# A gated cross-attention, feed-forward and slot-expert block: half of the slots attend among the experts' products

## The chip, the cores and the metric

The kernel runs on one core of a Trainium2 chip. The metric is the device time of one execution, in microseconds (us). Everything is float32. A core has five engines that run their own instruction streams in order: TensorE (PE in the profile; PEld is its weight load), VectorE (DVE), ScalarE (ACT), GpSimd (POOL) and SyncE (SP, which here only issues DMAs). Sixteen DMA engines move the data.

## The reference, cut to what matters

```python
# x, ctx: (8, 512, 512); 4096 tokens of width 512
x = x + tanh(g_xattn) * xattn(layernorm(x), ctx, mask)
x = x + tanh(g_ffn) * ffn(layernorm(x))

def xattn(x, context, mask):            # 16 heads of 64; keys and values shared by all heads
    xn, cn = layernorm(x) * gamma, layernorm(context) * ctx_gamma
    q, (k, v) = heads(xn @ Wq) / 8, split(cn @ Wkv)
    attn = softmax(where(mask == 0, -inf, q @ k.T))
    out = merge(attn @ v) @ Wout
    a, gate = split(xn @ Wff1)          # 2048 each
    return out + (silu(gate) * a) @ Wff2

def ffn(x):                             # 16 slots, one expert each, F = 2048
    q = broadcast(slot_query)
    o = q + mha(q, x, x)                # slots attend to the 512 tokens; 16 heads of 32
    h = layernorm(o)
    u, g = silu(h @ e_W1[slot] + b1), silu(h @ e_Wg[slot] + bg)
    o = o + (u * g) @ e_W2[slot] + b2
    return mha(x, o, o)                 # tokens attend to the 16 slots
```

## The kernel before

The eight batches of 512 tokens go through five stages, one after the other.

**A, cross-attention (lines 145 to 685).** A unit is a batch, a half of the heads and a block of 128 queries: 8 x 8 = 64 units, numbered by g. The loop of line 586 takes two steps (h) for a unit. `scores` multiplies keys with queries on PE (L292), takes the row maximum on DVE (L303), the exponential on ScalarE (L306) and normalises on POOL (L319). `turn_blocks` (L331) transposes 32x32 blocks on DVE, and one unit later `spread` (L335) moves the blocks to their partitions with sixteen DMAs of 128 KB on SP's queue; for the last two units every second one is on POOL's. `weigh` (L349) multiplies with the values, `add_out` (L365) with Wo. The keys of a batch are needed on both halves of the partitions: `place_keys` (L252) copies one half to the other by a DMA on SP (L258). Before the loop starts, for the first batch, the two loads of Wo (1 MB each, L557) stand ahead of that copy on SP. In the last batch there is no next batch to prepare, and PE takes steps of `carried_queries` (L379) instead: it folds the slots' queries with their key weights into the tile qt.

**B, feed-forward (lines 699 to 1052).** Products of combined blocks (L806, L830), with combinations made by POOL and DVE. Its first loads (xs, w1g, w1a; L737 to L744) are on SP, behind the last `spread`.

**C, the slots attend (lines 1111 to 1264).** 16 slots x 16 heads make 256 rows of queries in qt, two blocks m = 0, 1 of 128 rows. For each batch: `turn_tokens` (16 transposes on PE, copied to the tile places[b] by ScalarE and DVE), `slot_scores` for each m (four matmuls with 512 columns, then DVE's maximum, ScalarE's exponential, DVE's reciprocal, POOL's normalising), `turn_probs` (four transposes for each m, copied by ScalarE), `slot_pool` (16 matmuls of 256 columns). After the last batch, 64 small and 4 large matmuls per output (L1254, L1261) make o for all 128 rows (slot, batch).

**D, the experts (lines 1268 to 1456).** 16 experts, each with 8 pieces of 1 MB of W1 and Wg (4 matmuls on each) and 4 pieces of W2 (4 matmuls): 192 pieces. `fetch` (L1077) issues the next piece on SP as soon as a piece's matmuls free its buffer. There are RING = 8 buffers that are filled in stage C, and MORE = 2 that come free at its end. The products of an expert are small on PE: all eight batches' slot makes 8 rows, padded to 32. Beside them run the tokens' queries of stage E: `token_queries` (L1346), 128 steps of one matmul with 512 columns, one after each piece of W1 and Wg from the second expert on. The order on PE is written out by hand: `open_expert` (biases), `expert_in`, `turn_hidden` of the expert before, `gate` on ScalarE and DVE, `expert_out` of the expert before, with `close_group` every fourth expert.

**E, the tokens attend to the slots (lines 1466 to 1597).** Starts when the last expert is in.

Each engine takes its instructions in the order of the program; PE cannot pass a step that waits.

Of the kernel before, what the change touches and what calls it, by code (L numbers as in the profile page):

```python
# [26 lines left out]
P = 128  # L28
# [10 lines left out]
NS = 16  # L39
NE = 16  # L40
# [9 lines left out]
def flamingo_block(  # L50
# [45 lines left out]
    qt = const.tile([P, ND, FH * NS], F32, name="qt")  # L96
# [48 lines left out]
    with ExitStack() as sa, tc.manual_schedule(engines=ALL_ENGINES):  # L145
# [106 lines left out]
        def place_keys(b, kp, made):  # L252
            kT = a2.tile([P, N], F32, tag="kT", name=f"kT_{b}")
            v = a2.tile([P, NT, XD], F32, tag="v", name=f"v_{b}")
            nc.scalar.copy(kT[0:XD, :], kp[0:XD, :])
            vT = a3.tile([P, N], F32, tag="cn", name=f"vT_{b}")
            nc.scalar.copy(vT[XD:P, :], kp[XD:P, :])
            nc.sync.dma_start(kT[XD:P, :], kT[0:XD, :])  # L258
            made["kT"] = kT
            yield  # L260
            tp = ps1.tile([P, NT, XD], F32, tag="turn", name=f"v_tp_{b}")
            for t in range(NT):
                nc.tensor.transpose(
                    tp[:, t, :], vT[XD:P, t * P : (t + 1) * P], ident[XD:P, XD:P]
                )
            nc.scalar.copy(v, tp)
            made["v"] = v
            yield
# [14 lines left out]
        def scores(b, u, pairs, qs, kT, bias, turned, behind):  # L283
# [39 lines left out]
            for l in pairs:  # L323
                for e in (0, 1):
                    behind.append((turned, 2 * l + e, prs[l, e]))
# [9 lines left out]
        def spread(b, u, turned):  # L335
# [3 lines left out]
            last = b == B - 1 and u >= UNITS - 2  # L339
            for k in range(4):  # L340
                for i in range(4):

                    queue = nc.gpsimd if last and i % 2 else nc.sync
                    queue.dma_start(  # L344
                        pT[32 * k : 32 * k + 32, :, i, :], src[32 * i : 32 * i + 32, :, k, :]
                    )
            return pT

# [30 lines left out]
        def carried_queries():  # L379
# [27 lines left out]
            bdq = a4.tile([P, 4, 4, NS], F32, tag="xn", name="bdq")  # L407
            nc.vector.memset(bdq, 0.0)
            for r in range(4):
                s = slice(FD * r, FD * r + FD)  # L410
                nc.vector.tensor_tensor(bdq[s, :, r, :], qp[s], wide(dbqT[s], NS), ALU.add)
            yield
            for g in range(4):
# [7 lines left out]
                for c in range(ND):  # L421
                    nc.tensor.matmul(
                        tp[:, c, :], lhsT=wkT[:, c * P : (c + 1) * P],
                        rhs=bdq[:, g].rearrange("p r s -> p (r s)"), start=True, stop=True,
                    )
                nc.vector.tensor_copy(qt[:, :, g * 64 : (g + 1) * 64], tp)
                yield
            tp = ps1.tile([P, 2], F32, tag="turn", name="bk_tp")
            for g in range(4):
                r0 = 64 * (g % 2)  # L430
                nc.tensor.matmul(
                    tp[r0 : r0 + 64, g // 2 : g // 2 + 1],
                    lhsT=bdq[:, g].rearrange("p r s -> p (r s)"), rhs=dbkT[:, g : g + 1],
                    start=True, stop=True,
                )
# [121 lines left out]
        for hp in range(2):  # L557
            nc.sync.dma_start(
                wo[:, hp * HP : hp * HP + HP], rows(Wout[hp * HP * P : (hp + 1) * HP * P, :])
            )  # L560
# [25 lines left out]
        for h in range(2 * (B * UNITS + 3)):  # L586
# [35 lines left out]
            if h == 1:  # L622
                next(kv)
            if h == 4:
# [5 lines left out]
            if k == 0 and to_spread is not None:  # L630
                sb_, su, st_, sv = to_spread
                to_weigh_next = (sb_, su, spread(sb_, su, st_), sv)
# [24 lines left out]
            if k == 1 and to_weigh is not None:  # L657
                for _ in weigh(*to_weigh, done):
                    pass
            if live and nb < B:  # L660
# [395 lines left out]
    RING, MORE = 8, 2  # L1056
# [5 lines left out]
    fetched = []  # L1062
    pieces = []
    for e in range(NE + 1):
# [4 lines left out]
        if e > 0:  # L1069
            for q in range(4):  # L1070
                pieces.append(("w2", e - 1, q))

# [4 lines left out]
    def fetch():  # L1077
# [3 lines left out]
        pool, tag = buffers[len(fetched) % (RING + MORE)]  # L1081
        t = pool.tile([P, 4, 512], F32, tag=tag, name=f"{kind}_{e}_{i}")
        fetched.append(piece)
# [14 lines left out]

# [6 lines left out]
    ball = slots.tile([P, 2, 256], F32, name="ball")  # L1105

# [3 lines left out]

    with ExitStack() as sc, tc.manual_schedule(engines=ALL_ENGINES):
        c1 = sc.enter_context(tc.tile_pool(name="c1", bufs=1, reuse_waits="tile"))
        c2 = sc.enter_context(tc.tile_pool(name="c2", bufs=2, reuse_waits="tile"))
        ps = sc.enter_context(tc.tile_pool(name="ps_c", bufs=2, space=PSUM, reuse_waits="tile"))

        dbo = c1.tile([P, D], F32, tag="mT", name="dbo")
        pooled = c1.tile([P, ND, FH, NS, B], F32, name="pooled")

        def load_norm(b):

            at = {2: 5, 3: 6, 4: 7, 5: B}.get(b)
            if at is None:
                y = c2.tile([P, NT, D], F32, tag="y", name=f"y_{b}")
# [17 lines left out]
        def slot_scores(b, m):  # L1141
            yT = places[b].rearrange("p (c n) -> p c n", c=ND)
            sp = ps.tile([P, N], F32, tag="sc", name=f"ssc_{b}_{m}")
            for c in range(ND):
                nc.tensor.matmul(  # L1145
                    sp, lhsT=qt[:, c, m * P : (m + 1) * P], rhs=yT[:, c, :],
                    start=(c == 0), stop=(c == ND - 1),
                )
                yield
            pr = c2.tile([P, N], F32, tag="pr", name=f"spr_{b}_{m}")  # L1150
            sums = c2.tile([P, 4], F32, tag="sums", name="ssums")
            mx, den, rden = (col(sums, i) for i in range(3))
            nc.vector.tensor_scalar(
                pr, sp, bk_rows[:, m : m + 1], None, ALU.add, ALU.max, accum_out=mx
            )
            nc.vector.tensor_scalar(mx, mx, -FSCALE, None, ALU.mult)
            nc.scalar.activation(pr, pr, AF.Exp, bias=mx, scale=FSCALE, accum_out=den)
            nc.vector.reciprocal(rden, den)
            nc.gpsimd.tensor_scalar(pr, pr, rden, None, ALU.mult)
            probs[b, m] = pr  # L1160
            yield

        def turn_probs(b, m):
            if m == 0:
                pTs[b] = c1.tile([P, NT, FH * NS], F32, tag="pT", name=f"spT_{b}")
            pr = probs.pop((b, m))
            tp = ps.tile([P, NT, P], F32, tag="tp", name=f"stp_{b}_{m}")
            for j in range(NT):
                nc.tensor.transpose(tp[:, j, :], pr[:, j * P : (j + 1) * P], ident)
            nc.scalar.copy(pTs[b][:, :, m * P : (m + 1) * P], tp)  # L1170

        def slot_pool(b):
            y, pT = ys.pop(b), pTs.pop(b)
            for half in range(2):
                pl = ps.tile([P, 2, FH, NS], F32, tag="pl", name=f"pl_{b}_{half}")
                for i in range(2):
                    c = 2 * half + i
                    for j in range(NT):
                        nc.tensor.matmul(  # L1179
                            pl[:, i], lhsT=y[:, j, c * P : (c + 1) * P], rhs=pT[:, j, :],  # L1180
                            start=(j == 0), stop=(j == NT - 1),
                        )
                nc.vector.tensor_copy(
                    pooled[:, 2 * half : 2 * half + 2, :, :, b].rearrange("p c h s -> p (c h) s"),
                    pl.rearrange("p c h s -> p (c h) s"),
                )

        ys, probs, pTs = {}, {}, {}
        ys[0] = load_norm(0)
        ys[1] = load_norm(1)  # L1190
        for _ in range(2):
            fetch()
        ys[2] = load_norm(2)
        for _ in range(RING - 2):
            fetch()
        nc.sync.dma_start(o, by_slot(slot_query[0]))
        nc.sync.dma_start(dbo, d_bo.partition_broadcast(P))
        ys[3] = load_norm(3)
# [4 lines left out]
        ys[4] = load_norm(4)  # L1203
        ys[5] = load_norm(5)

# [4 lines left out]
        for _ in slot_scores(0, 0):  # L1210
            pass
        for b in range(B):
            if b == B - 4:
# [4 lines left out]
            if b > 0:  # L1218
                turn_probs(b - 1, 1)
            late = slot_scores(b, 1)  # L1220
            for t in range(NT):
                next(late)
                if b + 1 < B:
                    turn_tokens(b + 1, t)
            next(late)
            if b > 0:
                slot_pool(b - 1)
            if b in (1, 2):
                ys[b + 5] = load_norm(b + 5)
            if b == 3:  # L1230
                nc.gpsimd.tensor_tensor(o, o, dbo, ALU.add)
# [3 lines left out]
            if b == B - 1:  # L1235
                dwo = c2.tile([P, 4, D], F32, tag="y", name="dwo")
                nc.sync.dma_start(dwo, rows(d_Wo))
            turn_probs(b, 0)
            if b + 1 < B:
                for _ in slot_scores(b + 1, 0):  # L1240
                    pass
        turn_probs(B - 1, 1)
        slot_pool(B - 1)


        mT = c1.tile([P, 4, P], F32, tag="mT", name="mT")
        op = ps.tile([P, D], F32, tag="sc", name="o_p")
        for g in range(5):
            if g < 4:
                mp = ps.tile([P, P], F32, tag="tp", name=f"mp_{g}")  # L1250
                for c in range(ND):
                    for r in range(4):
                        h = 4 * g + r
                        nc.tensor.matmul(  # L1254
                            mp[FD * r : FD * r + FD, :], lhsT=dwv[:, c, h * FD : (h + 1) * FD],
                            rhs=pooled[:, c, h].rearrange("p s b -> p (s b)"),
                            start=(c == 0), stop=(c == ND - 1),
                        )
                nc.vector.tensor_scalar(mT[:, g, :], mp, dbvT[:, g : g + 1], None, ALU.add)
            if g > 0:  # L1260
                nc.tensor.matmul(  # L1261
                    op, lhsT=mT[:, g - 1, :], rhs=dwo[:, g - 1, :], start=(g == 1), stop=(g == 4)
                )
        nc.vector.tensor_add(o, op, o)


# [370 lines left out]
```

## Time and profile before

| | us |
|---|---|
| median of 3 runs (2985.1 to 2985.89) | 2985.8 |
| the profiled execution | 2985.67 |
| its span, first to last instruction | 2983.6 |
| PE busy in the span | 2874.2 (96%) |
| DVE, POOL, ACT busy | 1771.5, 1052.9, 796.9 |
| moved by DMA | 483.39 MB, 162 GB/s in the mean |

| stage | from | to | us |
|---|---|---|---|
| A | 0 | 1053.9 | 1053.9 |
| B | 1053.9 | 2242.4 | 1188.5 |
| C | 2242.4 | 2389 | 147 |
| D | 2389 | 2858 | 469 |
| E | 2858 | 2983.6 | 126 |

The stages are read from the first instruction of each on PE. An average over the span tells little here, as the stages differ: a window over one stage gives what is full in it, and the chain of waits gives what each piece of work waited for last. In the profile's lists of PE, an fp32 matmul is two records, so "x8" is four matmuls. The middle ones of the durations are 0.862 us for a matmul with 512 columns, 0.432 with 256, 0.222 with 128 and 0.111 for a transpose of 128x128, counted from start to start where PE runs without a gap.

### The profile page before, as it was taken

Reading aid. Unit: us, or ns where it says so; the run is one execution under the profiler, and the core shown is the slowest. Engines: PE = TensorE matmul, PEld = TensorE weight load, DVE = VectorE, ACT = ScalarE, POOL = GpSimd, SP = SyncE. Lnnn points to the kernel's source line nnn. Section 1 sums busy time; section 2 is a strip of 40 time slices with the busy share of each in tenths; the row PEclk is TensorE's granted clock in tenths of the full one; section 3 lists DMA queues with packets and bytes.
Section 4 is the critical chain, followed back from the end, with each engine's and each line's share of the span. In section 5 each row is a group of like instructions: output and inputs, shape, how many; then the busy total and the mean of one; then the engine's idle time right before and its main releaser. Section 6 shows DMA issues by size and latency. Waiting matters only on the chain.

```text
span 2983.6 us, 46833 instructions
## 1 busy us (share of the span) xinstructions
PE 2874.2 (96%) x16286; PEld 1828.6 (61%) x16286; DVE 1771.5 (59%) x5296; ACT 796.9 (27%) x2202; POOL 1052.9 (35%) x851
## 2 busy tenths in 40 slices
PE   8999999999999999999999999999999988787899
PEld 5333333333333389999999999999996622222245
DVE  6887878878786676666666666666654310001045
ACT  4444444444444411111111111111112100000022
POOL 5888888878887780000000000000002100000034
PEclk9999999999999999999999999999999999999999
DMA  6987877778788750000000000000015199999954
GB/s 174 201 209 177 212 186 194 199 187 214 183 201 194 178 193 29 29 30 29 30 29 29 30 29 29 29 29 30 29 55 203 43 399 420 420 420 420 420 221 147
DMA packets 277404, 483.39 MB, mean 162 GB/s; under 512 B 26624, under 2 KB 197408, under 8 KB 251568
## 3 DMA queue, kind: packets, MB, share of 16 engines
q1 hardware_dynamic: 275616, 476.20, 50.7%
q0 software_dynamic: 1248, 3.67, 0.5%
q8 instruction: 129, 2.11, 0.3%
q14 instruction: 107, 0.88, 0.1%
q10 hardware_dynamic: 304, 0.53, 0.1%
HBM read 304.14 MB, written 40.89 MB: 116 GB/s over the span
## 4 chain that ended last, share of the span: by engine, by line
PE 79%; DMA 16%; DVE 2%; SPq 1%; issue 1%; POOL 1%; ACT 0%; DVEq 0%; ACTq 0%; POOLq 0%
PE p L806 26%; PE acc L830 13%; PE sim L292 8%; DMA wg<-in_L_ffn_e_Wg_dram 7%; PE av L355 7%; PE qp L275 7%; DMA w<-in_L_ffn_e_W_dram 7%; PE op L369 6%; PE out L1554 2%; PE pl L1179 2%; PE ssc L1145 2%; SPq L344 1%; PE sc L1523 1%; DMA pT<-turned 1%; PE tp L213 1%; PE kp L247 1%
## 5 line engine op out<-in xcount | busy, mean ns | idle before, releaser
L319 POOL TENSOR_SCALAR pr<-pr,rden 128x512 f32<-128x512 f32 x504 | 788.3, 1582 | 184.2 <-DVE rden L312 182.5
L306 ACT ACTIVATE pr<-pr,nmx 128x512 f32<-128x512 f32 x512 | 363.5, 711 | 380.7 <-DVE nmx L303 334.5
L303 DVE CUSTOM_DVE_ANT_0 pr<-sim,bias 128x512 f32<-128x512 f32 x512 | 322.9, 685 | 83.4 <-PE sim L292 83.4
L331 DVE STREAM_TRANSPOSE turned<-pr 128x512 f32<-128x512 f32 x512 | 327.3, 682 | 9.4 <-DMA pT<-turned 1.2
L806 PE MATMUL p<-xs,w1g 128*128 128x128 f32 x2048 | 312.7, 275 | 0.0
L806 PE MATMUL p<-ts,s 128*128 128x128 f32 x2048 | 311.8, 275 | 0.3 <-POOL s L791 0.3
L830 PE MATMUL acc<-w,ht 128*128 128x256 f32 x1024 | 305.9, 381 | 0.0
L806 PEld LDWEIGHTS p<-ts,s 128*128 128x128 f32 x2048 | 289.4, 192 | 13.4 <-POOL s L791 0.5
L806 PEld LDWEIGHTS p<-xs,w1g 128*128 128x128 f32 x2048 | 279.8, 192 | 6.4
L292 PE MATMUL sim<-kT,q 64*128 64x512 f32 x1024 | 267.6, 621 | 7.1 <-DMA kT<-kT 5.0
L858 POOL TENSOR_TENSOR xr_b<-xr_b,qa 128x256 f32<-128x256 f32 x16 | 11.7, 731 | 678.5 <-DVE xr_b L855 678.5
L1359 DVE TENSOR_SCALAR place<-tq,vec 128x512 f32<-128x512 f32 x32 | 24.0, 751 | 378.5 <-PE tq L1354 378.5
L275 PE MATMUL qp<-xnT,wq 128*128 128x512 f32 x496 | 248.0, 624 | 0.6 <-DVE xnT L235 0.6
L355 PE MATMUL av<-pT,v 128*64 128x512 f32 x1024 | 237.3, 606 | 4.1 <-DMA pT<-turned 2.2
L369 PE MATMUL op<-wo,o 128*128 128x512 f32 x512 | 230.8, 594 | 1.4 <-ACT o L361 1.4
L830 PE MATMUL acc<-t,ht 128*128 128x256 f32 x768 | 229.3, 381 | 0.0
L292 PEld LDWEIGHTS sim<-kT,q 64*128 64x128 f32 x1024 | 92.5, 187 | 173.9 <-issue 108.1
L1038 DVE TENSOR_TENSOR c<-p,w 128x128 f32<-128x128 f32 x256 | 74.7, 292 | 178.4 <-PE p L806 177.8
L275 PEld LDWEIGHTS qp<-xnT,wq 128*128 128x128 f32 x496 | 85.5, 192 | 154.8 <-issue 145.7
L1044 ACT ACTIVATE g<-g 128x128 f32<-128x128 f32 x256 | 79.4, 310 | 355.7 <-DVE g L1043 350.8
L1032 ACT ACTIVATE g<-p 128x128 f32<-128x128 f32 x256 | 70.9, 277 | 385.3 <-PE p L806 385.3
L369 PEld LDWEIGHTS op<-wo,o 128*128 128x128 f32 x512 | 95.4, 190 | 114.6 <-issue 112.4
(263 smaller groups left out, 4285.0 us busy)
## 6 DMA issues: line engine op xcount, KB each, us to landing
w<-in_L_ffn_e_W_dram SPq DMA_DIRECT2D x128, 1024.0 KB, 19.9
pT<-turned SPq DMA_DIRECT2D x1008, 128.0 KB, 2.8
wg<-in_L_ffn_e_Wg_dram SPq DMA_DIRECT2D x64, 1024.0 KB
wq<-in_L_xattn_Wq_dram SPq DMA_DIRECT2D x64, 256.0 KB, 4.5
xn<-in_x_dram SPq DMA_DIRECT2D x32, 256.0 KB, 3.2
cn<-in_ctx_dram SPq DMA_DIRECT2D x32, 256.0 KB, 3.5
xnT_kept<-xnT SPq DMA_DIRECT2D x8, 1024.0 KB
xr<-in_x_dram SPq DMA_DIRECT2D x32, 256.0 KB, 4.1
```

The costliest lines, as they stand in the source:

```text
L275: nc.tensor.matmul(qp, lhsT=w[:, c, :], rhs=xnT[:, c, :], start=(c == 0), stop=(c == ND - 1))
L292: nc.tensor.matmul(sps[l, e], lhsT=qs[half * HP + l][r, t * P : (t + 1) * P], rhs=kT[r, :], start=True, stop=True,)
L303: nc.vector.tensor_tensor_reduce(pr, sps[l, e], bias, -XSCALE, LARGE, ALU.add, ALU.min, nmx)
L306: nc.scalar.activation(pr, pr, AF.Exp, bias=nmx, scale=-1.0, accum_out=dens[l][:, e : e + 1])
L319: nc.gpsimd.tensor_scalar(prs[l, e], prs[l, e], rden[:, e : e + 1], None, ALU.mult)
L331: nc.vector.transpose(turned[:, :, hd, :], pr.rearrange("p (j c) -> p j c", c=32))
L355: nc.tensor.matmul(av[XD * e : XD * e + XD], lhsT=v[:, j, :], rhs=p5[:, j, :, :, e, :], start=(j == 0), stop=(j == NT - 1),)
L369: nc.tensor.matmul(op, lhsT=o[:, l, :], rhs=wo[:, half * HP + l, :], start=(l == 0), stop=(l == HP - 1),)
L806: nc.tensor.matmul(psum[:, 0:HN], lhsT=w[:, c, :], rhs=x[:, c, :], start=(first and c == 0), stop=(last and c == 1), skip_group_check=True,)
L830: nc.tensor.matmul(part(acc, q), lhsT=ht[:, idx, :], rhs=rhs, start=(kp == 0 and half == 0), stop=(kp == NFC // 2 - 1), skip_group_check=True,
L1038: nc.vector.tensor_tensor(c22, p7[:, 0:HN], w, ALU.add)
L1044: nc.scalar.activation(g2, g2, AF.Silu)
```

## The change

Four things are changed.

1. The first batch's copy of the keys is issued by ScalarE instead of SP, and the two loads of Wo move from before the loop to its steps h = 1 and 2.
2. The last unit of stage A is transposed by PE (`turn_last`: 32 transposes into the banks of the scores, 8 copies by DVE and ScalarE) instead of by DVE blocks and sixteen DMAs. The `spread` of the unit before is wholly on SP.
3. qt is laid out in halves of eight slots (HS = 8), with all 16 heads in each half. Stage C does m = 0 alone, all batches, and the output of its 64 rows; it also does the scores of m = 1 for batch 0.
4. The half m = 1 goes into stage D as a generator, `late_slots`. For each batch it scores, turns the tokens back from places[b] with 16 transposes (their other layout is gone by then), turns probabilities and pools; after the last batch it makes its 64 rows of o, their norm and their transposes. `advance` is called after every one of the 192 pieces (W2's included). It spreads the late steps evenly over the first SWITCH = 71 pieces, then frees the late slots' memory, loads the queries' weight cwq, and adds three buffers to the ring, and from LAG = 4 pieces later spreads the 128 query steps over the pieces up to LAST, five before the end. The ring is RING = 7 buffers, 10 after the switch. The accumulators p_w1, p_wg and yq of the experts have one PSUM bank each instead of two.

The diff, cut to its core:

```diff
         def place_keys(b, kp, made):
+            queue = nc.sync if b else nc.scalar
...
-            nc.sync.dma_start(kT[XD:P, :], kT[0:XD, :])
+            queue.dma_start(kT[XD:P, :], kT[0:XD, :])
...
-            last = b == B - 1 and u >= UNITS - 2
...
-                    queue = nc.gpsimd if last and i % 2 else nc.sync
-                    queue.dma_start(
+                    nc.sync.dma_start(
...
+        def turn_last(heads, pT):
+            for hd in heads:
+                tp = ps4.tile([P, NT, P], F32, tag="sim", name=f"pr_tp_{hd}")
+                for j in range(NT):
+                    nc.tensor.transpose(tp[:, j, :], last_prs[hd][:, j * P : (j + 1) * P], ident)
...
+                if hd % 2:
+                    nc.scalar.copy(dst, src)
+                else:
+                    nc.vector.tensor_copy(dst, src)
...
-        for hp in range(2):
-            nc.sync.dma_start(
-                wo[:, hp * HP : hp * HP + HP], rows(Wout[hp * HP * P : (hp + 1) * HP * P, :])
-            )
...
+            if h in (1, 2):
+                r0 = (h - 1) * HP
+                nc.sync.dma_start(
+                    wo[:, r0 : r0 + HP], rows(Wout[r0 * P : (r0 + HP) * P, :])
+                )
...
+            if h == 2 * B * UNITS - 1:
+                last_pT = big.tile([P, NT, 4, HH * 32], F32, tag="pT", name="pT_last")
+                turn_last(range(HH // 2), last_pT)
+            if h == 2 * B * UNITS:
+                turn_last(range(HH // 2, HH), last_pT)
...
-    RING, MORE = 8, 2
+    RING, MORE = 7, 3
...
+        def late_slots():
+            for b in range(B):
+                if b > 0:
+                    yield from slot_scores(
+                        b, 1, ps1.tile([P, N], F32, tag="sc", name=f"lsc_{b}")
+                    )
+                    yield from slot_pool(
+                        b - 1, ps1.tile([P, 4, P], F32, tag="pl", name=f"lpl_{b - 1}")
+                    )
...
+                for t in range(NT):
+                    tp = ps1.tile([P, ND, P], F32, tag=("qp", "lt")[t % 2], name=f"ltp_{b}_{t}")
+                    for c in range(ND):
+                        nc.tensor.transpose(tp[:, c, :], yT[:, c, t * P : (t + 1) * P], ident)
...
+                turn_probs(b, ps1.tile([P, 4, P], F32, tag="qp", name=f"lstp_{b}"))
+                yield
...
+        SWITCH, LAG, LAST = 71, 4, PIECES - 5
+        AHEAD = 3
...
+        def advance():
+            i = beside["used"] = beside["used"] + 1
+            if i <= SWITCH:
+                while beside["done"] * SWITCH < i * LATE_STEPS:
+                    beside["done"] += 1
+                    next(beside["late"])
+            if i == SWITCH:
...
+                nc.sync.dma_start(cwq, rows(c_Wq))
+                buffers[:0] = [(more, f"m{k}") for k in range(MORE)]
+                for _ in range(MORE):
+                    fetch()
...
+            if i > SWITCH + LAG:
+                while beside["done"] * (LAST - SWITCH - LAG) < (i - SWITCH - LAG) * 128:
+                    beside["done"] += 1
+                    next(beside["queries"], None)
...
-            act = [ps.tile([P, 512], F32, tag=nm, name=f"p_{nm}_{e}") for nm in ("w1", "wg")]
+            act = [ps1.tile([P, 512], F32, tag=nm, name=f"p_{nm}_{e}") for nm in ("w1", "wg")]
...
                     fetch()
-                    if e > 0:
-                        next(querying, None)
+                    advance()
...
                 fetch()
-                if e == NE - 2:
-                    next(querying, None)
-                    next(querying, None)
+                advance()
```

## The prediction

> **What bounds the kernel now.** I read the page's row of 40 slices first (each about 74.6 us), then windows over the stages, then the chain of waits, then PE's timeline at the edited places.
>
> ```profile
> PE   8999999999999999999999999999999988787899
> PEclk9999999999999999999999999999999999999999
> DMA  6987877778788750000000000000015199999954
> GB/s 174 201 209 177 212 186 194 199 187 214 183 201 194 178 193 29 29 30 29 30 29 29 30 29 29 29 29 30 29 55 203 43 399 420 420 420 420 420 221 147
> ```
>
> The stages show themselves: A up to slice 14 and B to slice 30 (PE full), then slices 30 and 31 are the slots' stage C (PE full, DMA row 5 and 1: nearly nothing moves), then D, the experts, where the DMA engines are full at 420 GB/s and PE has gaps, then E. The windows give it in us:
>
> ```profile
> 2250.00:2300.00 50.00, 49.53 (x217) 32.61 (x216) 17.32 (x44) 15.38 (x31) 10.95 (x8) 1.00 0.73 270
> 2300.00:2350.00 50.00, 49.90 (x218) 34.05 (x217) 19.36 (x40) 11.57 (x24) 10.80 (x8) 1.00 0.00 0
> 2400.00:2450.00 50.00, 44.14 (x284) 12.03 (x284) 6.92 (x10) 2.39 (x4) 1.64 (x2) 1.00 1.01 420
> 2450.00:2500.00 50.00, 41.03 (x255) 10.49 (x255) 3.47 (x5) 1.19 (x2) 0.00 (x0) 0.93 1.01 420
> 2480.00:2490.00 10.00, 7.84 (x57) 2.51 (x58) 0.00 (x0) 0.00 (x0) 0.00 (x0) 0.66 1.01 418
> ```
>
> Columns: busy PE, weight load, DVE, ACT, POOL, then PE's clock, DMA share, GB/s. C has PE at 49.9 of 50 and DMA at 0; D has DMA at 1.01 and PE at 41 to 44. So work taken from C and put into D leaves a stage that PE bounds for one that DMA bounds. The chain of waits says the same: matmuls only in C, one DMA after the other in D.
>
> ```profile
> 2355.40 3.44 PE ssc L1145 x8
> 2359.27 3.44 PE ssc L1145 x8
> 2362.71 6.91 PE pl L1179 x32
> ...
> 2405.61 18.30 DMA w<-in_L_ffn_e_W_dram
> ...
> 2835.62 19.90 DMA w<-in_L_ffn_e_W_dram
> ```
>
> A weight piece (1 MB) takes 19.9 us because 8 are in the queue: 2.497 us each (1 MB at 420 GB/s). D's first weight is used at 2391.6, its last lands at 2855.5: 463.9 us. I make the sum against the profiled execution, 2985.67 us (span 2983.6, 2.07 around it); the median of three, 2985.8, is the same to 0.13.
>
> **1. First keys by ScalarE, Wo later.** PE at the start:
>
> ```profile
> 26.67 1.12 PE L292 MATMUL sim<-kT,q 64*128 64x512 f32 x2
> 32.57 3.75 PE L292 MATMUL sim<-kT,q 64*128 64x512 f32 x6 [4.78 <-DMA kT<-kT]
> 36.24 6.11 PE L275 MATMUL qp<-xnT,wq 128*128 128x512 f32 x8
> ```
>
> The copy of the first keys, issued at 23.94, lands at 32.43, 8.49 us later, behind 2 MB of Wo issued at 19.93 on the same queue. PE stands 4.78 us, then runs at a low clock: 32.57 to 42.3 holds 6 and 8 records that take 1.6 and 3.6 us in the timeline nearby. Without the gap, the scores of step h=1 start at 27.8 + 5.2 = 33.0 instead of 42.29: **-9.3 us**. ScalarE issues the copy after its second half copy, about 24.5; at the 3 us which a lone 128 KB copy takes (page: 2.8) it lands at 27.6. Behind it ScalarE has only q's copies, and 0.6 us of issue is spare (ACT is busy 27%). Wo goes onto SP at h=1 and h=2, ahead of the first spread (about 45): 1 MB each, 5 us of DMA, first needed by the first output product far later. The sixteen issues behind it are late by at most that; before, DVE bounds this stretch (44.3 of 48 us busy in 44 to 92), so part of a gain here could be eaten: -5 to -10.
>
> **2. Last unit by PE.** Before, spread(63)'s sixteen DMAs take SP's and POOL's queues; the pieces of B's weights stand behind them and are issued at 1037 to 1039, land at 1050.18 (the chain: 11.53 us of DMA w1a), and PE waits 2.17 and 1.96 us for av(62) and av(63). Added: 32 transposes at 0.111 = 3.6 us of PE and 8 copies (0.58 ACT, 0.68 DVE) beside them, in the "sim" banks that no scores need any more. Removed: av(63)'s wait (1.96), the last half of the slow av(63) (5.35 instead of 3.65 = 1.7), and the late weights. Against it: spread(62) is now on SP alone, 16 x 0.62 = 10 us instead of half, so av(62) starts about a microsecond or two later. PE's work ahead of B then ends near 1052 instead of 1054.07: **-2 us**, -5 to +2. The combinations that POOL makes for B have a start at 1038 instead of 1050, but only a microsecond of B waited for them.
>
> **3. Half the slots in C.** Of a batch's PE work C keeps 4 score matmuls (0.862), 16 pooling ones at 128 columns (0.222, from the 128x128 rows of stage B) and 16 + 4 transposes (0.111): 3.45 + 3.55 + 2.22 = 9.22 us, instead of 8 x 0.862 + 16 x 0.432 + 24 x 0.111 = 16.5 (16.54 in the chain, from one pooling to the next). First batch 5.2, six times 9.22 = 55.3, the eighth without token turns 7.4, then the second half's first scores 3.45, last probabilities 0.44, their copy seen by PE 0.75, pooling 3.55, copy 1.1 and the output 6.8: 84.0 us from 2245.5, to 2329.5. Before, 2387.2: **-57.7 us**, +-3. Is the softmax short enough? DVE 0.83 + 0.15, ACT 0.91, DVE 0.16, POOL 1.57 = 3.7 us, and PE has 3.55 of pooling and three scores with three token turns (3.9 us) before it wants it: yes, by 3.7. The loads of y start as before; batch 2 must be there at 2250.7 and is, by under a us.
>
> **4. The other half in D.** *DMA:* the ring starts with 7 pieces and not 8 + 2, and Wq of the queries is loaded in D: four MB more land behind the first use, 4 x 2.497 = **+10.0**. *PE:* how a piece and one more step share PE is here:
>
> ```profile
> 2403.43 1.13 PE L1354 MATMUL tq<-place,cwq 128*128 128x512 f32 x2
> 2404.49 1.06 PE L1387 MATMUL p_wg<-wg,hT 128*32 128x512 f32 x8
> 2405.48 1.13 PE L1354 MATMUL tq<-place,cwq 128*128 128x512 f32 x2
> ```
>
> A piece and a query together 2.05 us, where each alone is 0.862: 0.33 for changing over. The late half is 28 scores 24.1, pooling 8 x 3.55 = 28.4, token turns 8 x 16 x 0.111 = 14.2, probabilities 3.6, output 6, h and o 0.9: 77.2 us. In the first 71 pieces that makes 71 x (0.862 + 0.33) + 77.2 + 17.5 (opening an expert, 1.75, and turning its hidden, 1.2, per 12 pieces) = 179.3, 2.525 a piece, against 2.497 of DMA: PE is the slower by **2 us** in all. A ring of 7 (17 us) covers single waits, not this mean. In the rest, 128 queries over 113 pieces: 1.13 x 0.862 + 1.19 + 0.25 = 2.41 a piece: DMA bounds by 3%. Cwq is issued at piece 71 behind the pieces in flight and wanted 4 pieces later; PE then has up to 7 pieces landed ahead, so waits little. *Waits in the row:* PE takes everything in order, so a late step that waits holds the next piece. Scores to probabilities' turn have 8 steps between (5 pieces, 13 us, for 3.7 of softmax); token turns alternate two banks, 0.6 to 0.7 us of copy for at least 0.86 of piece between. The banks of w1, wg and yq go from two to one: gate(e)'s reading (0.6 + 0.6) lies beside expert_out, except for expert 0, about 0.5 to 2 us. D: **+12.5**, +10 to +25.
>
> **The clock, row against rule.** In D before, the clock falls after each expert's output, where PE waits for weights:
>
> ```profile
> 2481.26 1.59 PE L1427 MATMUL yq<-w,held 128*32 128x512 f32 x8 [1.42 <-DMA w<-in_L_ffn_e_W_dram]
> 2483.75 1.93 PE L1427 MATMUL yq<-w,held 128*32 128x512 f32 x8 [0.90 <-DMA w<-in_L_ffn_e_W_dram]
> ```
>
> 8 records take 1.93 where 1.06 is normal. The waits for w2 are 45.8 us of PE in D. With work beside the w2 pieces too these waits go, and the clock should be 1.00 as in stage C. The Trainium skill speaks against it ("TensorE: Matmul & The Clock Gate", Part 1, on cycling through PSUM banks): micro-idles between groups throttle the clock again, and the change does halve the banks, and Part 4 there has transposes not count as busy. PE's whole work in D is 165.5 + 77.2 + 110.3 + 61 of changing over + 51 = 465 us. By the row, at 1.00, it lies under the DMA's 474 and D is +12.5; by the rule, at the 0.93 of before, 465 / 0.93 = 500 and D is +36, the total 2953. I take the row: C's clock was 1.00 with 24 transposes a batch in it. The rule's value goes into the range.
>
> **5. Tail, and the small edits.** Queries end 5 pieces before the weights do, so the last pieces run as before and E (2857 to 2983.6) keeps its 127 us. The layout of qt and eight small bk_tp matmuls for four (0.05 each) lie in A's last units: nothing, or 0.3 us without that cover. **0**, +-1.
>
> **Sum.** -9.3 - 2.0 - 57.7 + 12.5 = -56.5: 2985.67 - 56.5 = **2929 us**.
>
> **Rivals.** (a) D becomes PE's: waits in the row, or the clock at 0.93: about 500 us instead of 476, 2953. For it: PE at 98 to 101% of DMA's pace with no slack. Against: waits shrink when the queue is never dry. (b) The start's gain is swallowed: DVE and POOL are busy 44 and 43 of 48 us behind it, so PE's earlier start is only a longer wait. 2929 + 9 = 2938. Against: the chain runs through PE's scores here, DVE itself waits for them. (c) All goes to the DMA floor: full start, last unit -5, C -60, D +10: 2921. (d) Slower than before: the clock in D is throttled by steps that each wait for one bank. Price: D = 465 / clock. It costs all 69 us that the rest brings once D exceeds 463.9 + 69 = 533, at a mean clock below 0.87; at 0.85 it is 547 us, the total 3000. For it: 0.66 in the window shown, with waits of only 0.6 to 1.4 us each. Against: such waits came from a dry DMA, and a slower PE fills the ring, which ends them.
>
> **Numbers.** Forecast 0.60, (a) 0.22, (b) 0.08, (c) 0.06, (d) 0.04. A measurement tells 0.2%, 6 us, from no change. Only (d) is slower, and between (a) and (d) a sliver lies at no change: faster 0.94, same 0.02, slower 0.04. The range, 2915 to 2957, reaches from (c) to (a); outside it are (d), the far end of (a) and a stray.
>
> **What would show it.** Start: sim without a gap at 27.8, the scores of h=1 at 33. C: 9.2 us from pooling to pooling, D's first weights 58 us earlier than B's end would give before. D: GB/s a little under 420 in the first 180 us, 420 after, PEclk 1.00, PE's gaps gone; first weight to last landing about 476. E 127 us. Wrong would make it: late steps with idle ahead of them in D (a bank, a softmax), PEclk under 0.95 there, GB/s of 400 and less for all of D, or E longer.

## The result and the profile after

| | before | after |
|---|---|---|
| median | 2985.85 us (4 runs, 2985.1 to 2987.45) | 2938.3 us (4 runs, 2937.8 to 2938.95) |
| span of the profiled execution | 2983.6 | 2936.7 |

The ratio is 0.9836, 95% interval 0.9822 to 0.9851. The forecast was 2929 with a range of 2915 to 2957: the sign and the mechanism held, 9 to 10 us of the 56.5 did not come. The page of the changed kernel, the same rows as before:

```profile
PE   9999999999999999999999999999999999899989
PEclk9999999999999999999999999999999999999999
DMA  7977878778788650000000000000006399999954
GB/s 206 202 201 179 208 186 195 196 188 214 179 204 201 165 195 30 30 30 29 27 29 28 27 28 30 30 30 30 30 19 240 119 419 419 417 420 420 420 194 144
```

Slices are 73.4 us now. C is shorter by more than half a slice, D is as full of DMA as before (419, 420) and PE is at 9 there instead of 7 and 8, but for one 8: its gaps are filled. The windows show it in us (busy PE, weight load, DVE, ACT, POOL, clock, DMA share, GB/s):

```profile
2245.00:2305.00 60.00, 59.95 (x390) 45.85 (x389) 23.30 (x49) 16.13 (x33) 10.08 (x8) 1.00 0.55 206
2305.00:2330.00 25.00, 20.22 (x234) 12.96 (x232) 8.87 (x19) 1.87 (x4) 3.62 (x3) 0.93 0.14 43
2330.00:2380.00 50.00, 49.49 (x374) 22.31 (x374) 12.09 (x26) 12.71 (x20) 5.92 (x4) 1.00 0.95 389
2380.00:2430.00 50.00, 48.52 (x345) 22.04 (x344) 9.71 (x22) 13.15 (x20) 4.69 (x3) 1.00 1.01 419
2570.00:2620.00 50.00, 49.23 (x276) 14.16 (x276) 7.80 (x12) 2.76 (x5) 0.00 (x0) 1.00 1.01 421
2804.50:2809.00 4.50, 3.85 (x16) 1.98 (x16) 0.54 (x2) 0.37 (x1) 0.00 (x0) 0.50 1.05 385
```

In these windows of D PE is at 48.5 to 49.5 of 50 with its clock at 1.00, and the stream does not suffer. (Between them, around the wait for cwq at piece 71, the clock was 0.74 from 2505 to 2525.) Two rows are odd: the end of C (20.2 of 25), and the first microseconds after the last weight, with the clock at 0.50.

To see where the time went I cut both traces at the same events of PE, which are not quite the borders of the stages: the first slot score, the first product with an expert's weight, the start of the last one, the end.

| stretch, us | before | after | difference | forecast |
|---|---|---|---|---|
| A and B, to the first slot score | 2245.5 | 2233.8 | -11.7 | -11.3 |
| C, to the first expert's weight | 146.1 | 96.6 | -49.5 | -57.7 |
| D, to the last output product | 464.0 | 474.1 | +10.2 | +12.5 |
| E, from there to the end | 128.0 | 132.2 | +4.2 | 0 |
| span | 2983.6 | 2936.7 | -46.9 | -56.5 |

So the missing time lies in C (8.2) and E (4.2); D gave 2.3 back.

PE's timeline at the start has no gap any more, and h=1 begins at 31.35:

```profile
25.80 1.99 PE L296 MATMUL sim<-kT,q 64*128 64x512 f32 x8
27.72 3.70 PE L279 MATMUL qp<-xnT,wq 128*128 128x512 f32 x8
31.35 1.99 PE L296 MATMUL sim<-kT,q 64*128 64x512 f32 x8
```

C's chain of waits has its expected rhythm, 9.2 us from pooling to pooling, but a break at the end:

```profile
2257.61 3.57 PE pl L1195 x32
2261.19 0.86 PE ssc L1166 x2
...
2266.81 3.57 PE pl L1195 x32
...
2305.84 3.45 PE lsc L1166 x8
2309.41 0.77 DVE spr L1174 x2
2311.79 5.48 PE pl L1195 x32
```

The last pooling starts 2.5 us after the scores and takes 5.48 instead of 3.57. Before the change PE waited 0.78 us at this place, for the copy alone, and pooled at full clock (16 matmuls with 256 columns):

```profile
2370.14 1.08 ACT spT L1170 x2
2371.27 7.19 PE pl L1179 x32
```

The timeline of all engines of the changed kernel names the holder:

```profile
2309.12 0.60 PE L1188 MATMUL stp<-ident,spr 128*128 128x128 f32 x4
2310.45 0.72 ACT L1178 ACTIVATE spr<-spr,ssums 128x512 f32<-128x512 f32 x1 [6.33 <-DVE ssums L1177]
2311.08 0.19 ACT L1178 ACTIVATION_READ_ACCUMULATOR spr<-spr,ssums 128x1 f32 x1
2311.17 0.56 ACT L1189 COPY spT<-stp 128x512 f32<-128x512 f32 x1
2311.79 5.47 PE L1195 MATMUL pl<-spT,y 128*128 128x128 f32 x32 [2.07 <-ACT spT L1189]
```

The copy spT, for which PE stands, could go at 2309.7, when the transposes end. But ScalarE has the exponential of the late half's first scores ahead of it in its program, and that waits for DVE's maximum until 2310.45. After the idle the granted clock is at half from 2312.4 for 3.4 us. ScalarE's order holds PE at C's beginning too:

```profile
2239.89 1.28 ACT L1178 ACT_TABLE_LOAD   x1 [2.60 <-DVE ssums L1177]
2241.18 0.72 ACT L1178 ACTIVATE spr<-spr,ssums 128x512 f32<-128x512 f32 x1
2241.81 0.19 ACT L1178 ACTIVATION_READ_ACCUMULATOR spr<-spr,ssums 128x1 f32 x1
2241.90 0.56 ACT L1253 COPY place<-ytp 128x512 f32<-128x512 f32 x1
...
2242.52 1.12 PE L1166 MATMUL ssc<-place,qt 128*128 128x512 f32 x2 [3.26 <-ACT place L1253]
```

The last token copy of the second batch, transposed by PE at 2238.66, is taken at 2241.90, behind the first exponential with its wait and the load of its table; PE idles 3.26 us. Before, four more scores of the first batch covered this place, and PE waited at most 0.24 us at a time until the first pooling.

```profile
2245.52 4.56 PE L1145 MATMUL ssc<-place,qt 128*128 128x512 f32 x10 [0.68 <-ACT place L1137]
```

### The profile page after: what moved, and what is told of

It reads as the page before. It is cut to its first block, busy times and chain, and to the rows that moved or that the text cites. A ratio compares the mean times of both kernels' runs of the same rounds, so it can differ in the third digit from the quotient of the medians.

```text
span 2936.7 us, 47981 instructions
## 1 busy us (share of the span) xinstructions
PE 2883.8 (98%) x16854; PEld 1851.6 (63%) x16854; DVE 1785.1 (61%) x5321; ACT 820.8 (28%) x2233; POOL 1045.5 (36%) x837
## 4 chain that ended last, share of the span: by engine, by line
PE 89%; DMA 7%; DVE 2%; SPq 1%; issue 1%; ACT 0%; POOL 0%; DVEq 0%; ACTq 0%; POOLq 0%
PE p L840 27%; PE acc L864 13%; PE sim L296 8%; PE av L374 8%; PE qp L279 7%; PE op L388 7%; DMA wg<-in_L_ffn_e_Wg_dram 3%; DMA w<-in_L_ffn_e_W_dram 3%; PE out L1681 2%; PE tq L1435 2%; PE p_wg L1510 1%; PE p_w L1510 1%; PE yq L1549 1%; PE lpl L1195 1%; PE lsc L1166 1%; PE pl L1195 1%
## 5 line engine op out<-in xcount | busy, mean ns | idle before, releaser
L840 PEld LDWEIGHTS p<-ts,w1a 128*128 128x128 f32 x1024 | 154.3, 191 | 13.7 <-DVE c L1072 0.4
## 6 DMA issues: line engine op xcount, KB each, us to landing
pT<-turned SPq DMA_DIRECT2D x1008, 128.0 KB, 2.8
```

The lines of the kernel that those rows point to most:

```text
L840: nc.tensor.matmul(psum[:, 0:HN], lhsT=w[:, c, :], rhs=x[:, c, :], start=(first and c == 0), stop=(last and c == 1), skip_group_check=True,)
```

## The experiments

Theory after the result: D is set by the stream alone; C lost its time to ScalarE's order; E to a clock that falls because the queries stop five pieces before the end. Rivals: PE's late steps bound D; the missing time in C lies in matmuls or loads; E's clock is chance. Each set ran on its own chip, where the kernel before had 2989.3 (e1 to e4), 2990.1 (e5 to e8) and 2987.35 us (e9 to e12), so the pieces are compared by stretches of the traces, each of one execution. "Slots from" is the first slot score. The medians of e1 to e8 stand beside a changed kernel timed in another set.

| run | median, us | slots from | C | D | E |
|---|---|---|---|---|---|
| changed | 2938.3 | 2233.8 | 96.6 | 474.1 | 132.2 |
| e9, changed again | 2938.6 | 2233.5 | 96.6 | 474.5 | 132.0 |
| e1, keys on SP | 2945.3 | 2240.5 | 96.6 | 474.3 | 132.0 |
| e2, last unit by DMA | 2943.0 | 2237.7 | 97.9 | 474.4 | 132.5 |
| e3, queries to the end | 2938.3 | 2236.3 | 97.8 | 474.4 | 132.6 |
| e4, order in C | 2930.4 | 2231.9 | 90.3 | 474.4 | 132.1 |
| e5, no late work | 2935.3 | 2233.2 | 96.3 | 474.4 | 134.2 |
| e6, SWITCH 51 | 2965.9 | 2233.7 | 98.0 | 501.2 | 131.9 |
| e7, ring of 6 | 2943.7 | 2234.6 | 97.9 | 476.8 | 134.0 |
| e8, orders together | 2929.4 | 2233.2 | 89.2 | 473.7 | 131.2 |
| e10, before again (one run) | 2987.9 | 2247.0 | 146.1 | 464.7 | 128.0 |
| e11, values first | 2937.2 | 2234.8 | 96.6 | 472.9 | 128.8 |
| e12, all together | 2923.6 | 2233.1 | 88.3 | 474.3 | 126.2 |

The stretch to the slots alone differs by up to 4.4 us between kernels with the same stage A and B (2231.9 to 2236.3; the mean of the changed kernel and e3 to e8 is 2233.8); a difference under that is not read from one trace. Nearly all of that scatter lies in A: B, from its first product behind the last output of A to the first slot score, took 1190.6 to 1190.9 in each of them.

**The start undone (e1).**

```diff
-            queue = nc.sync if b else nc.scalar
+            queue = nc.sync
...
+        for hp in range(2):
+            nc.sync.dma_start(
+                wo[:, hp * HP : hp * HP + HP], rows(Wout[hp * HP * P : (hp + 1) * HP * P, :])
+            )
...
-            if h in (1, 2):
...
```

> The changed kernel with its first part undone: the first keys' copy is on SP again, behind both loads of Wo. If the wait at the start is carried through to the end, the 9.3 us of the prediction come back: about 2947.5 (2944 to 2949). If DVE and POOL would have swallowed the earlier start, the time stays within 2 us of 2938.3.

```profile
25.80 1.12 PE L296 MATMUL sim<-kT,q 64*128 64x512 f32 x2
30.86 3.75 PE L296 MATMUL sim<-kT,q 64*128 64x512 f32 x6 [3.94 <-DMA kT<-kT]
34.54 5.96 PE L279 MATMUL qp<-xnT,wq 128*128 128x512 f32 x8
40.43 1.99 PE L296 MATMUL sim<-kT,q 64*128 64x512 f32 x8
```

The wait and the half clock are back, h=1 starts 9.1 us later (40.43 against 31.35), the slots 6.7 us later than the mean, the median is 7 above, within the range expected. So about 7 of 9 us are carried through; whether some 2 are swallowed in between, the scatter does not tell. The run undoes the queue and the place of Wo together, so which of the two was needed stays open.

**The last unit undone (e2).**

```diff
-                    if (b, u) == (B - 1, UNITS - 1):
-                        last_prs[2 * l + e] = prs[l, e]
-                    else:
-                        behind.append((turned, 2 * l + e, prs[l, e]))
+                    behind.append((turned, 2 * l + e, prs[l, e]))
...
+                    queue = nc.gpsimd if last and i % 2 else nc.sync
...
-            if h == 2 * B * UNITS - 1:
...
```

> The changed kernel with its second part undone: the last unit of stage A goes through DVE's block transposes and sixteen DMAs again, half of those of the last two units on POOL's queue. Prediction's term: 2 us back, about 2940.3. In the trace B starts 11.2 us earlier than before the change, so if the start gave the whole 9.3 there are 1.9 left for this part; if the start gave less, this part gives more, up to 6.

The median is 4.7 above the changed kernel's (2938.4 to 2946.0). The slots start at 2237.7, 3.9 after the mean: 1.2 before B, which is within the scatter, and 2.7 within it, which is not. There the weights land late, and PE waits for POOL's combinations:

```profile
1052.99 0.71 PE L831 MATMUL p<-ts,s 128*128 128x128 f32 x4 [0.93 <-POOL s L816]
```

6.7 + 3.9 = 10.6 is near the 11.7 of the table, but the run is not the old kernel again. In the two traces of before, B takes 1191.7 and 1192.4, only 0.8 to 1.5 longer than after the change: the weights are there 3.5 us ahead of B's products (POOL starts at 1050.35, B at 1053.85), in e2 1.6 us (1042.70 and 1044.28). And both traces of before have half clock under one of the last two products with the values (5.35 instead of 3.65 us), which e2 has not. What the second part gave is therefore known only as some 1 to 4 us.

**Queries to the end (e3).**

```diff
-        SWITCH, LAG, LAST = 71, 4, PIECES - 5
+        SWITCH, LAG, LAST = 71, 4, PIECES
```

> LAST is PIECES in place of PIECES - 5: the token queries go on to the last piece. Theory: the last pieces left PE idle, its clock was halved for the last output, y_tp and the first key product, and stage E lost about 4.2 us after the last weight had landed (132.2 against 128.0 before the change). With queries to the end the clock stays up: 2934 to 2935. Rival: stage E is later for its own reason (the loads of the residual, the zeroing of bdk on ScalarE) and the time stays at 2938, or rises as the last queries stand ahead of E's work.

A miss: no gain, 2938.3. In the trace the clock holds to the last piece (its product takes 1.06 instead of 1.94 us), but the last query's copy stands ahead of the output's on DVE, the first key product begins 4.3 us after the last product (4.7 in the changed kernel, 3.0 before), and the clock then falls after all: 0.77 from the first key product to the first value product. (The trace is of the slowest of the four runs, 2942.9.) The loss moved. This leaves the cause open; e10 to e12 take it up.

**The order in C (e4).**

```diff
                 if t == NT - 1 and b > 0:
                     turn_probs(b - 1, bank4("tp", f"stp_{b - 1}"))
+                if b == 0:
+                    turn_tokens(b + 1, t)
                 next(late)
-                if b + 1 < B:
+                if 0 < b < B - 1:
                     turn_tokens(b + 1, t)
...
-        probs_7 = probs.pop(B - 1)
-        for _ in late:
-            pass
-        probs[B - 1], probs_0 = probs_7, probs.pop(0)
+        for _ in range(3):
+            next(late)
         turn_probs(B - 1, bank4("tp", f"stp_{B - 1}"))
+        next(late)
+        probs_0 = probs.pop(0)
```

> Two orders in stage C changed: the second batch's tokens are turned ahead of the first batch's score matmul, so that their copy on ScalarE is not behind the first exponential, and the last batch's probabilities are turned one matmul earlier, so that their copy is not behind the late half's exponential. Theory: ScalarE in order cost 3.3 us at the first place and 2.1 + 1.9 (half clock) at the second; of the first, some 1.5 us turn into a wait for the first softmax, which still loads its table. Total gain 5.5 to 7: about 2932. Rival: the 8 us missing in C lie in the pooling matmuls or in loads, and the order brings under 1 us.

C falls from 96.6 to 90.3, the time to 2930.4. At the end PE's timeline now runs on:

```profile
2303.84 0.60 PE L1188 MATMUL stp<-ident,spr 128*128 128x128 f32 x4
2304.28 1.02 PE L1166 MATMUL lsc<-place,qt 128*128 128x512 f32 x2
2305.17 1.05 PE L1195 MATMUL pl<-spT,y 128*128 128x128 f32 x7
```

The copy is done beside the last score, and pooling follows on it. Two places where nothing but the order of the steps changed hold 6.3 of the 8.2 us that C fell short of: 2.2 at the first (first score to first pooling, 14.4 to 12.2) and 3.8 at the second (start of the seventh batch's pooling to the output, 16.4 to 12.6). Part of it is the clock: with the changed kernel's order every trace has 3.4 to 6.8 us of half clock in C, at one of the places or both, and with the order of e4, e8 and e12 none has any.

**No late work (e5).** The body of the loop over batches in `late_slots` is replaced by 100 empty steps, with only its output and norm left.

> The late half's scores, token turns, probabilities and pooling are left out of stage D (its rows are made from the first half's pooled values); all pieces, their order and the ring stay. Theory of the DMA floor: D is 186.5 MB of stream after the first weight plus a few us, so from the first weight to the last landing it stays 471 to 474 us, and the total falls by at most 2 us, but PE idles and its clock falls. Theory that PE's late steps bound D: the first 71 pieces get 10 us or more shorter.

```profile
2380.00:2430.00 50.00, 28.63 (x204) 5.48 (x200) 2.52 (x4) 2.39 (x4) 0.00 (x0) 0.85 1.01 420
```

PE has 20 us of 50 free, its clock is 0.85, and D is 474.4 as with the work in it. In D the late half is free: it stands wholly beside the stream. (The median is 3 us lower, a little more than expected; the trace, of the slowest of the four runs, 2939.9, cannot show where.)

**SWITCH 51 (e6).**

```diff
-        SWITCH, LAG, LAST = 71, 4, PIECES - 5
+        SWITCH, LAG, LAST = 51, 4, PIECES - 5
```

> SWITCH is 51 in place of 71: the same 109 late steps beside 51 pieces, the queries beside the rest. PE per piece in the first part by the prediction's sum: 0.862 + 0.33 + 77.2/51 + 0.25 = 2.96 us against 2.497 of the stream, so the first part takes 151 instead of 127 us and the stream, which a ring of 7 throttles, loses about 20 us: 2956 to 2960. If the stream alone set D's time whatever PE does beside it, it stays at 2938.

```profile
2380.00:2430.00 50.00, 47.63 (x375) 25.31 (x375) 12.94 (x25) 14.44 (x22) 4.69 (x3) 1.00 0.93 342
2430.00:2480.00 50.00, 47.43 (x452) 24.96 (x450) 9.98 (x20) 9.38 (x15) 3.12 (x2) 1.00 0.93 354
```

PE is busy no more than at 71 pieces, but the stream is down to 342 and 354 GB/s: 1 MB every 3.0 us or so, near the 2.96 of the sum. D is 27 us longer, what was lost is not made up, and the time is 2965.9, 6 above the expected range; that rest was not followed. So at 71 pieces PE's work just fits, at 51 the stream waits for PE. Where between them the cover ends was not run.

**A ring of 6 (e7).**

```diff
-    RING, MORE = 7, 3
+    RING, MORE = 6, 4
```

> The ring starts with 6 buffers in place of 7, with 4 more in place of 3 after the switch. By the prediction's term of 2.497 us per MB that is not there when D begins: +2.5 us, 2940.8. If also the steadiness of the stream suffers with 15 us of cover in place of 17.5: 2943 or more. If D is not bound by the stream: no change.

D is 476.8, 2.3 to 2.65 more than in the traces with a ring of 7 and all the work (474.1 to 474.5) for one MB less ahead of its start, against 2.497 expected. The median, 2943.7, is some 3 us higher than that. It is not the stream's steadiness: in the trace (2945.1; the runs lie between 2939.2 and 2945.2) C is 1.3 and E 1.9 longer, and in each the clock is at half for 3.4 us more than in the changed kernel's.

**Orders together (e8).** e3 and e4, and this:

```diff
-                    if t % 2:
+                    if t % 2 or b == 0:
                         nc.scalar.copy(dst, tp)
```

> The orders of e4 and the queries of e3 together, and the first late steps' copies in D on ScalarE alone, so that DVE's norm of the slots is not behind them (1.5 us from the output of C to the first weight). If the parts add: -6 - 4 - 1.2, about 2927. If a gain in C is eaten by D's stream, that starts only with its first weight, less; the stream does not wait for anything else, so all should be kept.

2929.4: C 89.2, another 1.1 for the third order, as expected; E is 131.2, so the queries bring about 1 us at most.

**Where E's time went (e9 to e11).**

> The changed kernel as it is, beside the versions of this set on one chip, for a time to hold them against: 2938 to 2942. Its stage E again 131 to 134 us from the last weight's product to the end, if the half clock there is its rule and not the chance of one execution.

> The kernel before, for a second trace of its stage E. Theory that the change itself makes E longer (PE idles beside the last pieces): again 128 us at clock 1.00 after the last weight. Theory that the clock falls there by chance of the moment, in either kernel: 130 or more in this trace, with a clock under 0.8 in the first 12 us after the last weight.

E is 132.0 in the changed kernel again and 128.0 in the kernel before again: not chance. What PE does ahead of it differs. The changed kernel's timeline (of its first trace):

```profile
2797.09 1.07 PE L1549 MATMUL yq<-w,held 128*32 128x512 f32 x8 [0.93 <-DMA w<-in_L_ffn_e_W_dram]
2799.48 1.07 PE L1549 MATMUL yq<-w,held 128*32 128x512 f32 x8 [1.32 <-DMA w<-in_L_ffn_e_W_dram]
2801.97 1.06 PE L1549 MATMUL yq<-w,held 128*32 128x512 f32 x8 [1.43 <-DMA w<-in_L_ffn_e_W_dram]
2804.50 1.94 PE L1549 MATMUL yq<-w,held 128*32 128x512 f32 x8 [1.46 <-DMA w<-in_L_ffn_e_W_dram]
2806.93 1.92 PE L1483 MATMUL y_tp<-fold,ys 128*128 128x32 f32 x8 [0.49 <-ACT ys L1479]
2809.23 6.17 PE L1606 MATMUL k_p<-oT,cwk 128*128 128x128 f32 x32 [0.38 <-DVE oT L1487]
```

and the kernel before at the same place:

```profile
2851.51 2.78 PE L1427 MATMUL yq<-w,held 128*32 128x512 f32 x24 [0.60 <-DVE held L1418]
2855.57 1.07 PE L1427 MATMUL yq<-w,held 128*32 128x512 f32 x8 [1.27 <-DMA w<-in_L_ffn_e_W_dram]
2857.12 1.09 PE L1340 MATMUL y_tp<-fold,ys 128*128 128x32 f32 x8 [0.49 <-ACT ys L1336]
2858.59 3.84 PE L1479 MATMUL k_p<-oT,cwk 128*128 128x128 f32 x32 [0.38 <-DVE oT L1344]
```

Before, two queries after each piece of the expert before had kept PE behind the stream: three pieces lay ready and only the last was waited for. In the changed kernel PE is level with the stream, idles before each of the last four pieces, and then does the last product, y_tp and most of the keys' products at half clock. These three lines take 10.0 us against 6.0 before, which is nearly all of the 4.2.

```diff
-            kp = ps.tile([P, 2, NS, B], F32, tag="mm", name=f"{name}_p_{half}")
+            kp = ps.tile([P, 2, NS, B], F32, tag="mm" if name == "k" else "out", name=f"{name}_p_{half}")
...
         slot_side(cwk, bdk, cbkT, "k", 1)
+        slot_side(cwv, bdv, cbvT, "v", 0)
+        slot_side(cwv, bdv, cbvT, "v", 1)
...
-            if i == 0:
-                slot_side(cwv, bdv, cbvT, "v", 0)
-                slot_side(cwv, bdv, cbvT, "v", 1)
```

> Of the changed kernel only stage E's opening is altered: the products for the slots' values follow at once on those for the keys, in banks of their own, so that PE does not idle while VectorE and ScalarE place the keys. Theory: the waits there (0.2 + 1.5 in the trace, 0.8 + 1.1 at full clock) and the clock that falls with them go: E 132 to 129, total 3 us less than the changed kernel in this set. Rival: the clock falls with the waits for the last weights, ahead of this place, and only 1 us is to be had.

E is 128.8 in the trace, which is of the fastest run (2934.8); the medians differ by 1.3 (2937.2 against 2938.6), less than the expected 3. The keys still take 5.44 us: the clock fell ahead of the last two products, was back for y_tp, and fell again under the keys, after waits that this edit does not touch.

**All together (e12).** e4, e8's third order, e11, LAST = PIECES - 1, and a one-element exponential at C's start that loads ScalarE's table.

> The orders of e8 with the queries up to one piece before the end, the values first, and the exponential's table loaded at the start of stage C instead of at its first softmax. Against the changed kernel in this set: C -7.4 and another -1 for the table, E -3: 11 us less. If the clock takes E's share again, 8.5 us less.

```profile
2795.67 1.06 PE L1553 MATMUL yq<-w,held 128*32 128x512 f32 x8 [0.45 <-DMA w<-in_L_ffn_e_W_dram]
2797.23 1.09 PE L1487 MATMUL y_tp<-fold,ys 128*128 128x32 f32 x8 [0.49 <-ACT ys L1483]
2798.70 3.84 PE L1610 MATMUL k_p<-oT,cwk 128*128 128x128 f32 x32 [0.38 <-DVE oT L1491]
2802.37 3.74 PE L1610 MATMUL v_p<-oT,cwv 128*128 128x128 f32 x32
```

2923.6 us (2922.2 to 2926.0, 5 runs; 0.9786 of before, 0.9773 to 0.9799), 15 less than the changed kernel beside it, more than the 11 expected: C 88.3, E 126.2. Neither kind of edit at E had brought its gain alone. With the queries up to the last piece (e8) the clock holds through the keys (3.84 us) and falls in the waits behind them; with the values first (e11) it falls ahead of them. Here both are filled, and the clock holds to the end. (The queries up to one piece before the end were not run without the values first.) It is the fastest version tried.

## Why the prediction was right, and where it fell short

- **The start, -9.3.** The mechanism was as told, and h=1 started at 31.35 where 33.0 was said. By e1 6.7 to 7 us arrive: within the range given (-5 to -10), perhaps with a part of rival (b) in it.
- **The last unit, -2.** 3.9 by e2, of which only the 2.7 in B are clear of the scatter. The prediction let POOL's late combinations count for a microsecond of B; that is what the two traces of before show (0.8 and 1.5), the 2.7 are e2's own. The term fits, its size is not settled. That A and B together came to -11.7 against -11.3 is in part luck.
- **C, -57.7 +-3.** This is the step that failed: -49.5, outside its own range. The count of matmuls was right (9.2 us from pooling to pooling). Two terms of the sum were not: "First batch 5.2" was 8.7, and "their copy seen by PE 0.75, pooling 3.55" was 2.2 and 5.5 with the cold clock. The question "Is the softmax short enough?" was answered for the chain of one batch, with free engines. It was not asked what else stands in ScalarE's program between: copies that PE waits for, behind exponentials that wait for DVE. e4 shows both places at 6.3 us together; the opening of D, where DVE's first late copy stands ahead of the norm, holds 1.1 (e8).
- **D, +12.5.** Measured +10.2, the +10.0 of four more MB; one MB is 2.3 to 2.65 (e7). The 2 us for a PE slower than the stream did not come, and e5 shows that with no late work D is no shorter. The sum's 2.96 us a piece for e6 is near what its stream shows (3.0), so PE's price per piece was about right; it was high by a little for 71.
- **The wait for cwq**, "waits little", was 6.09 us of PE at 2513. cwq took 12.0 us from its issue at 2507.0, and PE was through the pieces ahead of the first query in 6, just because they lay ready. It cost next to nothing, since the stream ran on (410 GB/s there, against 420).
- **The clock.** The row was right against the rule for D: with single banks and transposes it was at 1.00 in D but for 10 us around the wait for cwq, and rival (a)'s 2953 did not come. But the tail, "0, +-1", was +4.2, from the same clock at a place where I had looked only at the work: "the last pieces run as before" was wrong, because before the queries had kept PE behind the stream there. "E longer" stood among the prediction's signs of being wrong, and it came.

## What to carry to other kernels

When half of a stage's work on the bound engine goes, what that work covered comes to light: list for each engine, in its program's order, what now stands ahead of each copy that the bound engine waits for. Work moved beside a stream is free up to the stream's pace per piece and costs in full beyond it; count PE's time per piece, and the megabytes that are no longer there at the start. Where an engine has to start at full speed on data that land last, give it work until that moment and right behind it: filling one gap of two brought 1.3 us or nothing in the medians here, both together some 6 us of stage E.

## What the runs showed of the hardware that was not expected

The clock fell to 0.50 in the fourth of four waits of 0.9 to 1.5 us, one every 2.5 us, no idle stretch being longer. The Trainium skill ("TensorE: Matmul & The Clock Gate", "Why this matters for your kernels") advises against idle gaps of more than about 3 us between bursts of matmuls; here several shorter ones, one after the other, were enough, and the measurement decides. In e5, with PE idle 20 us of 50, the mean clock was 0.85.

The traces say more of what counts. The granted clock changes in steps of 3.41 us (it stays at half for 3.41, 6.83, 10.24 or 13.65), and the share of PE's work in the step ahead seems to decide. Ahead of this fall PE was busy 1.11 of 3.41 us, ahead of the one in e8's stage E 1.56. In the kernel before, the same waits behind the keys lie differently across the steps (2.58 and 2.41 busy), and the clock held. So the stop of 3.26 us at C's beginning lies mostly in one step in e3 (1.17 busy; the clock fell) and is shared by two in the changed kernel (1.96 and 1.60; it held). Counted over all fourteen traces from 2200 us on, 59 of 69 falls follow a step with PE busy under 45%, and of the 2858 steps behind which full clock went on, none was below that. This is read from the records; no run varied the share alone, and ten falls came at a higher share.

And a stream of 1 MB loads kept 419 to 421 GB/s whether PE was busy 57% or 98% beside it.
